# Layer 0 of a four-layer graph network: a bias, a fetch, a count array and an output stage are placed differently

## The chip, the cores and the metric

The kernel is one program on one core of a Trainium2 chip. The metric is device time in microseconds (us) of one execution, the median of several runs. Engines are named as in the profile: PE (TensorE matmuls; PEld are its weight loads), DVE (VectorE), ACT (ScalarE), POOL (GpSimd), SP (SyncE, which only issues transfers). Any of SP, ACT and POOL can issue a DMA, and each works its instructions off in order.

## The reference

The whole is four layers over 3125 nodes with 256 features and 103125 edges (50000 random ones, their reverses and 3125 loops). Only layer 0 is touched by the change. It adds an edge attention (8 heads of 32) and a linear mixer to x, then a mixture of 8 experts of which each node takes its best two:

```python
xn = _layernorm(x, axis=-1)
x = x + gnn(xn, edge_index, Wp, a_src, a_trg, Wskip, bias) + mix(xn, Wqkv, ..., bproj, ...)
x = x + ffn(_layernorm(x), gamma, beta, Wr, br, W1, b1, W2, b2)

def gnn(x, ...):
    proj = (x @ Wp.T).reshape(-1, H, FO)
    s = leaky_relu(scores_src[src] + scores_trg[trg], 0.2)
    attn = exp(s) / (segment_sum(exp(s), trg)[trg] + 1e-16)
    out = segment_sum(proj[src] * attn[:, :, None], trg)
    return elu((out + (x @ Wskip.T).reshape(-1, H, FO)).reshape(-1, H * FO) + bias)
def mix(x, ...):
    ...
    return out * gate @ Wproj + bproj
def ffn(x, ...):
    xn = (x - mu) * rsqrt(var + 1e-05) * gamma + beta
    logits = xn @ Wr + br
    top_vals, top_idx = top_k(logits, 2)
    ...
    h = gelu(xn @ W1[e] + b1[e]); y_e = h @ W2[e] + b2[e]
```

## The kernel before

The nodes are 25 tiles (NT) of 125 (TP = 125 partitions); x, xn and xT stay in SBUF (N = 3125, C = 256, P = 128, KC = 2). GROUPS are seven groups of 4, 4, 4, 4, 3, 3, 3 tiles; `part_dma` splits every transfer by partitions in two. Layer 0 runs in these stages.

**Preparation** (0 to 102 us). `run` loads x in four parts, in turns over SP and ACT; `begin` normalises and transposes group by group; `prepare` projects each group for the attention and, at group 3, calls `edges()`, which turns the sorted edge list into keys (`is_key`, `seg_d` in DRAM).

**Counts** (102 to 377). The graph is turned into a dense table: how many edges run from each source node to each target node. `counts` makes 63 steps: DVE compares keys to two one-hot tables (`oh_lo` L1734, `oh_key` L1737), PE multiplies these (`p_cnt` L1750), ACT evicts the sums to `stage` (L1752) or, for the targets in FAR, also to `far` (L1755). Each block of 250 targets is written to the DRAM arrays `count_d` (bytes, L1759) and `far_d` (bf16, L1762) by SP. BLOCKS is the order of the blocks. Between the steps, 93 pieces of the mixer are woven in (`mix0_pieces`): first node tables, then the fold (`fold_pieces`, which loads wkv at L1627), then for each group the gated output. Ahead of the groups POOL adds `bproj` to the whole of x at once (L1786).

**Attention loop** (`dense_pairs`, 387.7 to 1012.4). Every pair of nodes is weighed by its count. The instruction order is written out by hand (`manual_schedule`). A near step n handles one (block, head) unit and one of 25 source tiles (NS = 25): DVE makes `pt` from the row `q_here`, the source's scalar `bar` and the counts `a` in one instruction over 1000 targets (L1986), PE multiplies it with the sources' features (L2000). There are 16 units, that is 400 near steps: the 8 heads for target tiles 0 to 7, then the 8 heads for tiles 8 to 15. A far step m does the nine tiles 16 to 24 (FAR0) for a pair of heads without DVE: ACT computes leaky relu and exp (L2029, L2030), POOL multiplies by the counts (L2031), PE sums (L2045). There are 100 far steps, one for every four near ones. When a unit is through, its sums are evicted (L1965) and turned to node rows (`turned`, L1954 to 1960); after the eighth head of the first block `then` (`outputs0`) is put into the list `ends`. `piece()` advances the open `turns` and then `ends` by one yield in each near step. After the loop the other eight near tiles and the nine far tiles go through `outputs0` alone.

**Outputs** (`outputs0`). For each tile: Wskip and the skip bias on PE (helper `mm`, L740; the bias is a matmul of one row of ones with one row of bias), added to the attention on DVE (L2696), ELU (exp and relu on ACT L2700, L2701; then DVE L2688, L2689, which also brings the result into x), batch-norm statistics. For all tiles: a root on ACT (L2704), `xn` normalised on DVE (L2711) and written to DRAM, transposed on PE (L2717), scaled into xT on DVE (L2719), multiplied with Wr for 8 scores a node (L2727, two matmuls a tile), then the best two by DVE.

**Experts** (from 1114). `routed0_weights` loads W1, b1, W2, b2 (L2755, 2757, 2759, 2663) over ACT and SP; `route` sorts nodes by expert; `routed0` gathers xn's rows with POOL (L2782), multiplies, and scatters results (L2848). Then layer 1 starts.

## Time and profile before

| what | us |
|---|---|
| median of 7 runs | 5538.43 (5535.86 to 5552.24) |
| the profiled execution's own time | 5542.23 |
| its span in the trace | 5540.3 |

| stage (us from the span's start) | length | PE busy | DVE busy | ACT busy | POOL busy | granted clock |
|---|---|---|---|---|---|---|
| preparation, 0 to 102 | 102.0 | 70.17 | 66.69 | 26.34 | 13.54 | 0.88 |
| counts, 102 to 377 | 275.0 | 235.59 | 239.69 | 180.27 | 21.26 | 0.91 |
| attention loop, 387.7 to 1012.4 | 624.7 | 596.84 | 536.69 | 515.29 | 476.38 | 0.97 |
| last outputs, 1012.4 to 1114.1 | 101.7 | 80.57 | 52.21 | 18.65 | 0 | 0.52 |
| route, 1114.1 to 1146.7 | 32.6 | 12.69 | 19.26 | 0 | 7.36 | 0.50 |
| first 238.3 us of the experts | 238.3 | 232.72 | 134.49 | 37.89 | 106.80 | 0.99 |

How to read it: the table's lines are busy times of engines by stretch, and "granted clock" is the TensorE clock that the throttle allowed, as a share of full speed. A line of the timeline in the text below has start, duration, engine, program line, operation, output<-inputs, shape, how many such instructions were put together, and in square brackets how long the engine was idle before it and what it then waited for. A line of the waits gives the waiting engine and line, what it waited for, and total us, number and longest. A line of the groups gives engine, operation, shape and count, then busy us and mean ns of one, then the idle time before.

### The profile page before, as it was taken

The numbers are of one execution on the slowest core, as the hardware profiler recorded it, in microseconds if no ns is written. First come the engines' busy times: TensorE is split into PE (matmuls) and PEld (weight loads), VectorE is DVE, ScalarE is ACT, GpSimd is POOL, SyncE is SP. The second block draws the span as 40 slices with busy tenths as digits, with TensorE's granted clock in tenths as the row PEclk, the third lists the DMA queues.
The fourth block names the chain that finished last, engine by engine and source line by source line (L and its number), as shares of the span: only waits on it lengthen the run. The fifth ranks groups of instructions, "written<-read, shape, count | busy, mean of one in ns | idle before, by whom it ended". The sixth has DMA issues, their size and how long they took to land. (4 is left out here: it accounts for less than half of the span.)

```text
span 5540.3 us, 68126 instructions
## 1 busy us (share of the span) xinstructions
PE 4836.3 (87%) x24840; PEld 2897.2 (52%) x24840; DVE 3530.0 (64%) x5869; ACT 1575.4 (28%) x2503; POOL 1520.8 (27%) x1398
## 2 busy tenths in 40 slices
PE   6889989889888999899998999999967668686768
PEld 4565434568444333686453334556645445454447
DVE  6978888555655998454448997323267666565643
ACT  3668868311421000101330001333311012222221
POOL 1118858234000000000100000000066556555533
PEclk8899999689899999999999999999978889888889
DMA  3865535412200111110001112000055455444535
GB/s 90 91 91 157 162 108 161 130 49 62 69 1 25 34 35 27 51 36 14 14 1 35 44 29 69 14 0 1 27 150 145 127 151 159 129 138 141 143 117 175
DMA packets 353191, 443.06 MB, mean 80 GB/s; under 512 B 144846, under 2 KB 273229, under 8 KB 352278
## 3 DMA queue, kind: packets, MB, share of 16 engines
q1 hardware_dynamic: 264514, 219.66, 16.4%
q0 software_dynamic: 53744, 171.34, 10.8%
q10 hardware_dynamic: 34593, 47.63, 2.8%
q8 instruction: 202, 3.31, 0.2%
q14 instruction: 138, 1.13, 0.1%
HBM read 384.86 MB, written 56.78 MB: 80 GB/s over the span
## 5 line engine op out<-in xcount | busy, mean ns | idle before, releaser
L2289 POOL DMA_INDIRECT z_edge<-tab,src_i x806 | 771.3, 957 | 535.2 <-issue 214.6
L1905 DVE SCALAR_TENSOR_TENSOR pt<-q_head,bar,a 128x750 f32<-128x750 f32 (+2 forms) x800 | 776.6, 1027 | 62.2 <-PE acc L2135 53.6
L2130 PE MATMUL acc<-pt,zs 128*64 128x375 f32 (+2 forms) x3200 | 603.5, 501 | 24.0 <-DVE pt L1905 23.8
L2357 PE MATMUL p_acc<-z_edge,oh 128*125 128x264 f32 x2044 | 557.4, 435 | 41.0 <-DVE z_edge L2348 25.4
L2031 POOL TENSOR_TENSOR pt_far<-pt_far,a_far 128x1125 f32<-128x1125 f32 (+1 forms) x200 | 476.4, 2383 | 279.8 <-ACT pt_far L2030 248.6
L2357 PEld LDWEIGHTS p_acc<-z_edge,oh 128*125 128x125 f32 x2044 | 435.8, 217 | 142.1 <-DVE z_edge L2348 28.0
L1986 DVE SCALAR_TENSOR_TENSOR pt<-q_here,bar,a 128x1000 f32<-128x1000 f32 (+1 forms) x384 | 456.0, 1250 | 40.2 <-DMA a<-count_d 18.0
L2130 PEld LDWEIGHTS acc<-pt,zs 128*64 128x64 f32 (+1 forms) x3200 | 246.9, 136 | 357.2 <-issue 220.8
L2000 PE MATMUL p_n<-pt,zs 128*64 128x500 f32 (+1 forms) x1600 | 402.8, 597 | 26.4 <-DVE pt L1986 25.7
L1278 DVE SCALAR_TENSOR_TENSOR x<-p_y,sm,x 125x256 f32<-125x256 f32 x200 | 96.7, 483 | 364.5 <-PE p_y L740 364.5
L2135 PE MATMUL acc<-pt,zs 128*32 128x375 f32 (+2 forms) x3200 | 313.4, 497 | 0.0
L2348 DVE TENSOR_TENSOR z_edge<-z_edge,near_e 128x2112 f32<-128x2112 f32 (+1 forms) x101 | 236.6, 2342 | 120.1 <-ACT near_e L2340 71.4
L2324 PE MATMUL p_e<-ident,m_sb 128*128 128x128 f32 x202 | 52.3, 348 | 282.2 <-ACT m_sb L2319 185.0
L2185 PE MATMUL acc<-zs,pt 128*125 128x257 f32 x1250 | 275.8, 383 | 11.6 <-DMA a<-count_d 11.6
L2185 PEld LDWEIGHTS acc<-zs,pt 128*125 128x125 f32 x1250 | 234.8, 189 | 52.6 <-issue 14.4
L2000 PEld LDWEIGHTS p_n<-pt,zs 128*64 128x64 f32 (+1 forms) x1600 | 159.2, 137 | 183.8 <-issue 79.1
L2029 ACT ACTIVATE pt_far<-q_log,log_s 128x1125 f32<-128x1125 f32 (+1 forms) x200 | 244.8, 1224 | 32.7 <-PE p_f L2045 30.7
L2045 PE MATMUL p_f<-pt_far,zs 128*64 128x375 f32 (+1 forms) x1200 | 242.6, 489 | 7.9 <-POOL pt_far L2031 7.8
L2030 ACT ACTIVATE pt_far<-pt_far,log_s 128x1125 f32<-128x1125 f32 (+1 forms) x200 | 247.0, 1235 | 6.5
L1262 ACT ACTIVATE h<-p_tr,bn 128x500 f32<-128x500 f32 (+1 forms) x224 | 161.8, 723 | 299.4 <-PE p_tr L740 299.4
L2319 ACT ACTIVATE m_sb<-p_m 128x256 f32<-128x256 f32 x101 | 38.8, 384 | 711.1 <-remote 350.5
L2302 DVE TENSOR_TENSOR hot<-row,near 125x1024 f32<-125x1024 int16 (+1 forms) x149 | 158.6, 1083 | 78.5 <-remote 64.6
(550 smaller groups left out, 7841.5 us busy)
## 6 DMA issues: line engine op xcount, KB each, us to landing
a<-count_d SPq DMA_DIRECT2D x384, 125.0 KB
a_far<-far_d SPq DMA_DIRECT2D x96, 281.2 KB
row<-dst_row SPq DMA_DIRECT2D x101, 224.0 KB
a<-count_d SPq DMA_DIRECT2D x144, 93.8 KB
ef<-in_edge_s SPq DMA_DIRECT2D x101, 128.0 KB
z_edge<-tab,src_i POOLq DMA_INDIRECT x806
count_d<-stage SPq DMA_DIRECT2D x12, 781.2 KB
q_head<-q_g ACTq DMA_DIRECT2D x24, 375.0 KB
```

The source lines that it names most:

```text
L1905: self.nc.vector.scalar_tensor_tensor(pt[:K, :n], q, bar, a[:K, :n], op0=OP.max, op1=OP.mult)
L1986: nc.vector.scalar_tensor_tensor(pt[:K], q[:K], bar[:K, t, h:h + 1], a[:K].rearrange("p (j n) -> p j n", j=2), op0=OP.max, op1=OP.mult)
L2000: nc.tensor.matmul(accs[u][64 * j:64 * j + 64, :M * TP], zs[:K, t, h * W:h * W + 64], pt[:K, j, :], start=(t == 0), stop=(t == NS - 1))
L2029: nc.scalar.activation(f[:K], logs[u, i][:K], AF.Relu, bias=log_s[:K, 0, t, h])
L2030: nc.scalar.activation(f[:K], f[:K], AF.Exp, bias=log_s[:K, 1, t, h], scale=1.0 - 0.2)
L2031: nc.gpsimd.tensor_tensor(f[:K], f[:K], a[:K], OP.mult)
L2045: nc.tensor.matmul(far_accs[u][b][64 * i:64 * i + 64, :n], zs[:K, t, z:z + 64], fs[i][:K, b * n:(b + 1) * n], start=(t == 0), stop=(t == N ...
L2130: nc.tensor.matmul(acc[i // 2][64 * (i % 2):64 * (i % 2) + 64, b, :b1 - b0], zs[:K, t, i * W:i * W + 64], pts[i][:K, b0:b1], **st)
L2135: nc.tensor.matmul(acc[2][32 * i:32 * i + 32, b, :b1 - b0], zs[:K, t, z:z + 32], pts[i][:K, b0:b1], **st)
L2185: nc.tensor.matmul(acc[i], pt[:K, i * TP:(i + 1) * TP], zs[:K, t, :C + 1], start=(t == 0), stop=(t == NS - 1))
L2289: nc.gpsimd.indirect_dma_start(out=zs[i][:, j, :], out_offset=None, in_=table, in_offset=bass.IndirectOffsetOnAxis(ap=src[:, c0 + j:c0 + j ...
L2357: nc.tensor.matmul(acc[t], ohs[i, t][:, k - a, :], zs[i][:, k - c0, :HW], start=(k == cols[t][0]), stop=(k == cols[t][1] - 1))
```

## The change

- x is loaded in the seven GROUPS, and `edges()` is called at the last group.
- BLOCKS has another order; `count_d` becomes three DRAM arrays of 1000, 1000 and 1125 targets (PARTS), so that a load of counts spans one or more arrays; the last block's counts are written by ACT's queue, not SP's.
- wkv is fetched within the node pieces, ahead of the weights that follow them.
- The addition of `bproj` to all of x goes; instead `shift = bproj - 1` is added to x tile by tile, on POOL, one tile in each of the first 25 far steps (`ahead`). The -1 is that of ELU, so that `outputs0` adds xn to x without it.
- The skip bias is a matmul of 128 rows: one row of bias and 127 of zeros, against 128 rows of ones.
- A far step comes every 3.5 near steps; the far tiles' `outputs0` joins `ends` inside the loop, and `ends` advance only in every third near step while far steps remain (`rare`).
- In `outputs0` normalisation and scaling into xT move from DVE to ACT, and the scores are computed as 8 rows by up to 500 nodes, evicted to `side` by ACT, and transposed back.
- Several pools have `reuse_waits="tile"` (waits for reused memory by tile); the experts' W1 is loaded over POOL's queue, b1, W2 and b2 over SP's.

```diff
-BLOCKS = [8, 0, 9, 1, 10, 2, 11, 3, 12, 4, 5, 6, 7]
+BLOCKS = [8, 0, 1, 9, 2, 10, 3, 4, 11, 5, 12, 6, 7]
+PARTS = ((0, 1000), (1000, 2000), (2000, N))
...
     def gnn0_weights(self, c):
...
+        bias = c.tile([P, C], F32, name="bias_row")
+        nc.gpsimd.memset(bias, 0.0)
+        nc.scalar.dma_start(bias[:1], dview(self.ins["L0_gnn_bias"], 0, [[0, 1], [1, C]]))
+        shift = self.row(c, "L0_mix_bproj")
+        nc.vector.tensor_scalar(shift, shift, -1.0, None, op0=OP.add)
...
-                if group == GROUPS[3]:
+                if group == GROUPS[-1]:
                     found = edges()
...
-        self.count_d = self.dram.tile([NS, P, N], U8, name="count_d")
+        self.count_d = [self.dram.tile([NS, P, b - a], U8, name=f"count_d{i}") for i, (a, b) in enumerate(PARTS)]
...
-                    nc.sync.dma_start(self.count_d[:, :, d0:d0 + nd].rearrange("t p d -> p t d"), stage[:, :, :nd])
+                    part = min(d0 // 1000, 2)
+                    c0 = d0 - PARTS[part][0]
+                    (nc.scalar if step == steps - 1 else nc.sync).dma_start(
+                        self.count_d[part][:, :, c0:c0 + nd].rearrange("t p d -> p t d"), stage[:, :, :nd])
...
-            for _ in self.node_pieces(nodes[:3], "g0", xT, 8, 0.2, w, ps, nodes[3:]):
+            for i, _ in enumerate(self.node_pieces(nodes[:3], "g0", xT, 8, 0.2, w, ps, nodes[3:])):
+                if i == len(GROUPS) + NS:
+                    wkv = self.keys_weight(w, "gate")
                 yield
...
-            nc.gpsimd.tensor_add(x, x, bproj[:, None, :].to_broadcast([TP, NT, C]))
...
-        nc.sync.dma_start(a[:K, :n], self.count_d[t, :K, d0:d0 + n])
+        for part, (c0, c1) in zip(self.count_d, PARTS):
+            b0, b1 = max(c0, d0), min(c1, d0 + n)
+            if b0 < b1:
+                nc.sync.dma_start(a[:K, b0 - d0:b1 - d0], part[t, :K, b0 - c0:b1 - c0])
...
-                        ends.append(then(we, ps_t, c, nn))
+                        ends.append(then(we, ps_e, c, nn))
...
+                    if 2 * u + 2 == H:
+                        ends.append(then(we, ps_e, f0, nf))
...
-                    if m <= NF and n >= 4 * m:
+                    if m <= NF and n >= 3.5 * m:
...
+                        if m < NT:
+                            ahead(m)
                         m += 1
...
-                    piece()
-                while turns or ends:
+                    piece(n % 3 and m <= NF)
+                while turns:
                     piece()
                 in_loop.close()
-                last = s.enter_context(tc.tile_pool(name="dapl", bufs=8, space=PSUM, reuse_waits="tile"))
-                ends = [then(we, last, n0 + nn, nn), then(we, last, *FAR0)]
+                banks.append(room("dapl", 7, space=PSUM))
+                ends.append(then(we, ps_e, n0 + nn, nn))
                 while ends:
                     ends = [e for e in ends if next(e, self) is not self]
...
-                self.mm(ys[k], [(xT[:, i, t * TP:(t + 1) * TP], wskip[:, i, :]) for i in range(KC)] + [(self.ones[:1, :TP], bias)])
+                self.mm(ys[k], [(xT[:, i, t * TP:(t + 1) * TP], wskip[:, i, :]) for i in range(KC)] + [(self.ones[:, :TP], bias)])
...
-                nc.vector.scalar_tensor_tensor(x[:, t, :], xn[:, t, :], -1.0, x[:, t, :], op0=OP.add, op1=OP.add)
+                nc.vector.tensor_add(x[:, t, :], x[:, t, :], xn[:, t, :])
...
+        nc.vector.scalar_tensor_tensor(off[:, :nt], mv[:, :nt, 0], -1.0, rstd[:, :nt], op0=OP.mult, op1=OP.mult)
...
-                nc.vector.tensor_scalar(xn[:, t, :], x[:, t, :], mv[:, k, 0:1], rstd[:, k:k + 1], op0=OP.subtract, op1=OP.mult)
+                nc.scalar.activation(xn[:, t, :], x[:, t, :], AF.Identity, bias=off[:, k:k + 1], scale=rstd[:, k:k + 1])
...
-                nc.vector.tensor_scalar(xT[:, k, (t0 + a) * TP:(t0 + a + na) * TP], p[:, :na * TP], g[:, k:k + 1], b[:, k:k + 1],
-                                        op0=OP.mult, op1=OP.add)
+                nc.scalar.activation(xT[:, k, (t0 + a) * TP:(t0 + a + na) * TP], p[:, :na * TP], AF.Identity, bias=b[:, k:k + 1], scale=g[:, k:k + 1])
...
-        for t in range(nt):
-            self.mm(p[:, t, :], [(xT[:, k, (t0 + t) * TP:(t0 + t + 1) * TP], wr[:, k, :]) for k in range(KC)])
+            p = ps.tile([P, 512], F32, name="p_o")[:E, :na * TP]
+            self.mm(p, [(wr[:, k, :], xT[:, k, (t0 + a) * TP:(t0 + a + na) * TP]) for k in range(KC)])
...
+            nc.scalar.activation(side[32 * i:32 * i + E, :na * TP], p, AF.Copy)
...
+        for u in range(each):
+            nc.tensor.transpose(p[:, u, :], side[:, u * TP:(u + 1) * TP], self.ident)
...
-                (nc.sync if e % 2 else nc.scalar).dma_start(w1[:, k, :, e, :], ins["L0_ffn_W1"][e, k * P:(k + 1) * P].rearrange("p (i f) -> p i f", i=2))
+                nc.gpsimd.dma_start(w1[:, k, :, e, :], ins["L0_ffn_W1"][e, k * P:(k + 1) * P].rearrange("p (i f) -> p i f", i=2))
...
-            nc.scalar.dma_start(b1[:, i], dview(ins["L0_ffn_b1"], i * C, [[0, P], [2 * C, E], [1, C]]))
+            nc.sync.dma_start(b1[:, i], dview(ins["L0_ffn_b1"], i * C, [[0, P], [2 * C, E], [1, C]]))
...
-            (nc.scalar if e % 2 else nc.sync).dma_start(w2[:, :, e, :], ins["L0_ffn_W2"][e].rearrange("(k p) f -> p k f", p=P))
-        return w1, w2, b1, self.matrix_rows(c, "L0_ffn_b2")
+            nc.sync.dma_start(w2[:, :, e, :], ins["L0_ffn_W2"][e].rearrange("(k p) f -> p k f", p=P))
+        return w1, w2, b1, self.matrix_rows(c, "L0_ffn_b2", nc.sync)
...
-        for i, (t0, nt) in enumerate(((0, 4), (4, 4), (8, 8), (16, 9))):
+        for i, (t0, nt) in enumerate(GROUPS):
...
+                                 lambda t: nc.gpsimd.tensor_add(x[:, t, :], x[:, t, :], skip[-1]))
```

## The prediction

> **What bounds it now.** Read first: busy time and granted TensorE clock by stretches (columns: stretch; its length; busy us of PE, PEld, DVE, ACT, POOL with instruction counts; clock; DMA share; GB/s). All edits sit in layer 0: preparation 0 to 102 us, counts to 377, attention loop 387.7 to 1012.4, a serial tail to 1146.7, then the experts.
>
> ```profile
> 388.00:700.00 312.00, 302.62 (x1539) 151.74 (x1540) 265.01 (x255) 276.15 (x243) 258.62 (x108) 0.98 0.56 163
> 700.00:780.00 80.00, 72.29 (x318) 27.07 (x320) 70.87 (x90) 52.17 (x58) 42.38 (x18) 0.94 0.36 102
> 780.00:830.00 50.00, 43.95 (x210) 18.45 (x212) 43.94 (x54) 29.26 (x27) 27.43 (x12) 0.86 0.39 114
> 830.00:1012.00 182.00, 177.58 (x915) 85.61 (x913) 156.56 (x149) 157.01 (x139) 147.95 (x63) 1.00 0.50 146
> 1012.00:1018.00 6.00, 3.10 (x18) 1.57 (x14) 2.14 (x9) 1.52 (x3) 0.00 (x0) 0.92 0.50 153
> 1030.00:1050.00 20.00, 20.00 (x39) 10.35 (x38) 7.72 (x22) 4.47 (x11) 0.00 (x0) 0.50 1.01 329
> 1050.00:1072.00 22.00, 22.00 (x43) 11.49 (x42) 13.03 (x38) 6.45 (x16) 0.00 (x0) 0.50 0.00 0
> 1072.00:1080.00 8.00, 0.22 (x1) 0.00 (x0) 7.45 (x24) 3.46 (x7) 0.00 (x0) 0.50 0.00 0
> 1148.00:1152.00 4.00, 3.49 (x12) 2.43 (x12) 1.39 (x4) 0.70 (x1) 0.95 (x1) 0.72 0.11 34
> ```
>
> In the loop (first four rows) PE is full and DVE, ACT and POOL are close behind it. From 700 to 830 PE starves while DVE is full: there the first 8 output tiles run inside the loop. The next rows are the tail, where 17 output tiles run alone: PE is busy throughout at clock 0.50, from 1072 DVE works alone. At 1148, with the experts' 128-row matmuls, the clock rises again.
>
> Second, one tail tile in order of time:
>
> ```profile
> 1042.74 1.21 PE L740 MATMUL p_o<-r_L_gnn_bias,ones 1*125 1x256 f32 x2
> 1043.89 2.07 PE L740 MATMUL p_o<-w_L_gnn_Wskip,xT 128*125 128x256 f32 x4
> 1043.99 0.42 DVE L2696 TENSOR_TENSOR xn<-xn,p_o 125x256 f32<-125x256 f32 x1 [2.63 <-PE p_o L740]
> ```
>
> A tile costs 1.21 + 2.07, overlapped 3.14 us, and DVE waits 2.63 of it. So PE sets the pace there; the bias, one row deep, is over a third.
>
> Third, the counts stage and the loop's start, in order of time:
>
> ```profile
> 154.98 13.73 POOL L1786 TENSOR_TENSOR x<-x,r_L_mix_bproj 125x6400 f32<-125x6400 f32 x1 [49.31 <-DMA r_L_mix_bproj<-in_L_mix_bproj]
> 155.06 14.98 DVE L1737 TENSOR_TENSOR oh_key<-key_t,is_key 128x2520 bf16<-128x2520 bf16 x1
> ...
> 387.67 1.26 DVE L1986 SCALAR_TENSOR_TENSOR pt<-q_head,bar,a 128x1000 f32<-128x1000 f32 x1 [11.02 <-DMA a<-count_d]
> 392.74 8.26 DVE L1986 SCALAR_TENSOR_TENSOR pt<-q_here,bar,a 128x1000 f32<-128x1000 f32 x7 [3.81 <-DMA a<-count_d]
> ```
>
> One POOL addition of 13.73 holds a DVE comparison of 1.46 for 14.98. The loop's first two vector steps wait 11.02 and 3.81 for counts.
>
> Fourth, the waits of that stage (us, times, longest):
>
> ```profile
> DVE oh_lo L1734 <- PE p_cnt L1750: 12.7, 15, 5.3
> ACT far L1755 <- DMA far_d<-far: 12.2, 2, 6.7
> ```
>
> PE and DVE stall behind ACT, which waits until the single far buffer has been written out.
>
> Fifth, DVE groups (count | busy, mean ns): first inside the loop (690 to 826), then in the tail.
>
> ```profile
> L2689 DVE SCALAR_TENSOR_TENSOR x<-xn,x 125x256 f32<-125x256 f32 x8 | 11.4, 1424 | 0.3
> L2711 DVE TENSOR_SCALAR xn<-x,mv,rstd 125x256 f32<-125x256 f32 x8 | 10.8, 1409 | 0.0
> ...
> L2689 DVE SCALAR_TENSOR_TENSOR x<-xn,x 125x256 f32<-125x256 f32 x17 | 7.2, 425 | 0.6
> L2711 DVE TENSOR_SCALAR xn<-x,mv,rstd 125x256 f32<-125x256 f32 x17 | 5.9, 407 | 0.1
> ```
>
> Beside POOL the same operation takes 1424 instead of 425, 1409 instead of 407.
>
> **The sum, part by part.** Times are those of the profiled execution, 5542.2 (span 5540.3), 3.8 above the median 5538.4.
>
> Preparation: the edge work moves to the last group and x comes in 14 pieces, not 8. DVE sat idle for 6.62 before the edge data (56 to 62.8), with later layernorms queued behind it; these now fill it. But the edge work, 14.5 on DVE, comes nearer to the end. Bounds 0 (all back) and -15 (all of it off the chain); I take -6, about the idle alone. Six more x issues cost 0.35 to 0.8 each on SP and ACT, under transfers that take 15.
>
> Counts: DVE is busy 239.7 of 275, so it paces. Without the addition: -13.5, but PE has 36 us of work in the 36 us left between 150 and 200, so -11. The new block order puts two or three blocks between most far writes instead of two: half of the 12.7. The Wkv fetch moves a few pieces earlier on POOL's queue; behind it stand only small memsets, so nothing. Bounds -8 and -24; -17.
>
> Loop start: the loads of the first counts need not wait for the last write, which leaves SP for ACT. The mixer's last addition ends at 376.6, so at most 11.02 + 3.81 = 14.8 go; the 500 KB query row still shares the DMA engines with that write. Bounds -6, -14.8; I take -10.
>
> Loop: steady, four near and one far step take 5.25: near 0.84 of PE, far 1.89. At 3.5 near to one far, 25 far steps need of PE 87.5 x 0.84 + 25 x 1.89 = 121, and 11 for drains (100 near steps took 142.9 where 131.3 are worked): 132. ACT needs 25 x 2 x (1.224 + 1.235) = 123, 5.6 for near and 1.4 for far evictions, 2 for new rows: 132. POOL needs 119, and 13.7 more in the first round for the 25 additions: 133. With three engines equal I take 136; bounds 132, 143. Near steps 0 to 206: 320; 300 to 350: 78. Between, 94 steps: 146, plus the first outputs. These bring PE 17.5 (8 tiles of 1.65, transposes, scores), ACT 15 (ELU 0.84, norm 0.42, evictions 0.3 a tile, two table loads), DVE 31 of which 11 is waiting for POOL; against some 5, 5 and 30 free: +20 (bounds 5, 40), 166. The last 50 near steps have no far work: DVE 50 x 1.19, turns 3.8, nine far tiles of 1.85: 80. Together 644 against 624.7 - 3.8: **+23**. The normalisation on ACT takes away the 1409s; ACT has no slack for it, which is why I grant little.
>
> The Trainium skill ("SBUF — State Buffer", SBUF: two separate sides) says a DVE operation with two SBUF inputs and a GpSimd operation that reads SBUF lock each other out; that speaks against POOL additions in the loop. By it, all 25 of 0.55 could stand in DVE's way: 14 more. The rows allow less: the near step, with one operand in PSUM, takes 1250 beside a POOL that is 83% busy.
>
> Tail: far tiles go through their ELU part in the loop (28 of 53 pieces, after 16 for far and near turns and 6 for the next). Left: last turn 3.2; eight tiles at DVE's 0.41 + 0.40 + 0.43 + 0.43 + 0.18 = 1.85, with start and lag 19; far top-two 4.6; root with its table 2.3; ACT norms, transposes, evictions and score matmuls (two 500-wide pairs and four transposes for 14.3 of 8-wide ones) 10.5; top-two 4.5. Sum 44 where 1012.4 to 1114.1 is 101.7: -57, taken -56. PE hides under DVE only if the clock is full: 1.65 a tile; at half, 3.14 stays and the sum is 54, so -47. I take full, since the bias is now 128 rows deep and 128-row matmuls bring the clock back at 1148.
>
> By the Trainium skill ("TensorE: Matmul & The Clock Gate", What's actually happening) some 3.4 us of busy time restore full clock whatever the rows. The rows here contradict it: 42 us busy at 0.50. By the rule the bias edit would win no clock.
>
> Expert weights: the loads leave ACT for POOL (16) and SP (11). Before, the DMA had finished by 1050, 37 after issue. On POOL the nearest row is 512 KB issued at 216.7, used at 224.1: eight such are 59, and the first use comes about 74 after the loop. The gathers queue behind them on POOL and xn's writes behind the others on SP; at worst 10 late. Route's constants ready earlier: -1.5. In later layers 100 count loads are split in two, 0.3 us of SP each, under 4 us steps: nothing.
>
> Sum: -6 - 17 - 10 + 23 - 56 - 1.5 = -67.5: 5474.7, less 3.8: **5471**.
>
> **Rivals.** (a) The loop does not lengthen: PE's own sum, 596 busy before, grows by only some 10. Loop 0, total -90: 5448. Against it: ACT is already 88% busy.
> (b) Covers fail: clock stays half, preparation gains nothing, gathers late: -67.5 + 9 + 6 + 10 = -42: 5496. For it: the clock fell at 1017 after a mere 3 us of idle PE.
> (c) Slower: the far chain (ACT, POOL, PE in turn, four buffers) paces the loop and does not fill. The change decides for worse where a far step over the first 350 near steps exceeds 136/25 + 67.5/100 = 6.1 us. For it: 7.7 from 700 to 824 (16 far steps). Against: there DVE held near steps at 2.1, and elsewhere it ran at 5.7. At 6.4: +30, 5568.
> (d) The parts cancel, within 10.
>
> **Numbers.** Forecast 0.66, (a) 0.15, (b) 0.08, (c) 0.08, (d) 0.03. 0.2% is 11 us, about what a measurement here can tell. Low: loop 0, preparation -12, counts -20: -110, 5428. High: loop +45, tail -47, counts -11, preparation 0, start -6: -20, 5518. Both reach (a) and (b). Faster 0.89, same 0.03, slower 0.08.
>
> **What would show it.** No POOL addition of 13.7 and no 15 us comparison; first near step under 385; far steps near 5.4 and near-only steps at 1.2 at the end; ACT, not PE, ending the far waits; 45 to 55 from the last near matmul to route, clock near 1 there. Wrong if far steps exceed 6.1, if the tail stays above 80, or if counts still take 265.

## The result, and the profile after

The changed kernel takes 5580.08 us (median of 24 runs) against 5546.29 for the kernel before (61 runs): a ratio of 1.0057, 95% interval 1.0044 to 1.0069. It is slower by 0.6%, where 1.2% faster was forecast. Runs were made in several groups; in two of them, both on one chip, the edge attention of layer 3, which no edit touches, took 1044 to 1055 us (from its first gather to its last product), in the others, on other chips as far as the chip is on record, 1314 to 1345. So whole times are compared only within a group, as ratios to the kernel before, and stages are read from the profiles.

The profiled execution of the changed kernel has its own time 5579.92 and a span of 5578.1. Stages, in us, against the first profile before ("key comparison" is the DVE step that makes `oh_key`; near steps are counted from 0, and all times are starts):

| stage | before | after | difference | forecast |
|---|---|---|---|---|
| start to first key comparison | 121.1 | 107.6 | -13.5 | -6 |
| first to last key comparison (counts) | 246.2 | 261.6 | +15.4 | -17 |
| last key comparison to near step 10 | 36.5 | 34.6 | -1.9 | -10 |
| near step 10 to last near step | 604.0 | 674.1 | +70.1 | +23 |
| last near step to first expert matmul | 138.9 | 84.1 | -54.8 | -57.5 |
| sum, layer 0 to the first expert matmul | 1146.7 | 1162.0 | +15.3 | -67.5 |

The remaining 22.5 of the span's 37.8 lie behind layer 0. Layer 3 alone is 31.0 longer (1313.5 to 1344.5), the rest somewhat shorter. The kernel before, profiled three times, had 1313.5, 1055.4 and 1317.7 there, and with the bproj addition left out 1344.8, so this part is not read as an effect of the change. Layer 0 itself varies too: in eight further profiles at one far step for 3.5 near ones the first expert matmul came at 1157.2 to 1185.4, in three of the kernel before at 1140.7 to 1158.4. So the +15.3 is at the low end. Behind the first expert matmul, the eight profiles of the two groups with the short layer 3 lie within 8 of each other (4128 to 4136), the kernel before among them (4130). So layer 0 is where the 0.6% most likely comes from; no run separates it further.

Busy time and clock by stretches of the changed kernel (columns as before: stretch, length, busy PE, PEld, DVE, ACT, POOL, clock, DMA share, GB/s):

```profile
404.00:711.00 307.00, 289.85 (x1456) 131.10 (x1454) 251.14 (x230) 269.44 (x237) 273.74 (x132) 0.98 0.51 147
711.00:997.00 286.00, 259.11 (x1227) 100.84 (x1225) 224.08 (x240) 231.41 (x222) 203.72 (x88) 0.95 0.43 125
997.00:1078.00 81.00, 70.12 (x284) 24.01 (x282) 78.02 (x112) 14.48 (x30) 2.48 (x2) 0.96 0.30 79
1084.00:1102.00 18.00, 17.29 (x75) 10.86 (x75) 10.32 (x30) 13.49 (x28) 9.68 (x14) 1.00 1.00 327
1102.00:1114.00 12.00, 1.72 (x7) 0.89 (x6) 9.43 (x34) 4.86 (x10) 2.94 (x7) 0.67 1.07 370
1132.00:1150.00 18.00, 6.03 (x29) 3.98 (x29) 15.49 (x45) 0.99 (x1) 0.00 (x0) 0.50 0.00 0
```

The first row is the loop without outputs, the second with the first eight output tiles, the third the near steps that are left when the far steps are through. In neither of the first two is an engine full: PE has 0.94 and 0.91 of the time, where it had 0.97 before in the stretch without outputs and 0.90 and 0.88 in those with them. The last three rows are the tail: the clock is at 1.00 while the eight tiles run, then DVE works alone.

One tail tile in order of time, as before the change at 3.14:

```profile
1089.89 1.03 PE L742 MATMUL p_o<-w_L_gnn_Wskip,xT 128*125 128x256 f32 x4
...
1091.39 0.42 DVE L2716 TENSOR_TENSOR xn<-xn,p_o 125x256 f32<-125x256 f32 x1 [1.81 <-PE p_o L742]
...
1092.38 0.59 PE L742 MATMUL p_o<-bias_row,ones 128*125 128x256 f32 x2
```

Wskip takes 1.03 instead of 2.07, the bias, now 128 rows, 0.59 instead of 1.21, both at the full clock; the Wskip of successive tiles starts every 1.4 to 3.0.

Counts and loop start in order of time:

```profile
188.68 8.49 POOL L1883 COPY log_s<-es 128x200 f32<-128x200 f32 x1 [94.54 <-DVE es L1879]
...
205.88 0.83 POOL L1635 DMA_DIRECT2D gate<-in_L_mix_Wqkv  x1 [7.91 <-ACT far L1762]
...
213.63 5.29 PE L742 MATMUL p_a<-gate,xT 128*125 128x512 f32 x6 [7.09 <-DMA gate<-in_L_mix_Wqkv]
...
224.85 1.49 DVE L1741 TENSOR_TENSOR oh_lo<-lo_t,is_lo 128x2560 bf16<-128x2560 bf16 x1 [11.29 <-PE p_cnt L1757]
...
378.44 1.25 DVE L2002 SCALAR_TENSOR_TENSOR pt<-q_head,bar,a 128x1000 f32<-128x1000 f32 x1
391.30 1.26 DVE L2002 SCALAR_TENSOR_TENSOR pt<-q_here,bar,a 128x1000 f32<-128x1000 f32 x1 [11.60 <-DMA count_d<-stage]
```

The addition of 13.7 is gone, but a POOL copy of 200 columns lasts 8.49, the matrix "fetched ahead" is issued behind it and after 7.91 more of waiting, PE waits 7.09 for it and DVE 11.29 for PE. The first near step comes 9.2 earlier than before, and then the second waits 11.60.

The waits of the counts, and the groups of DVE and ACT, first inside the loop (715 to 1000), then in the tail:

```profile
DVE oh_lo L1741 <- PE p_cnt L1757: 22.6, 19, 11.3
...
ACT far L1762 <- DMA far_d<-far: 4.9, 1, 4.9
```

```profile
L2709 DVE TENSOR_TENSOR x<-x,xn 125x256 f32<-125x256 f32 x8 | 9.2, 1156 | 0.8
L2708 DVE SCALAR_TENSOR_TENSOR xn<-elu_e,xn 125x256 f32<-125x256 f32 x8 | 7.5, 936 | 0.0
L2736 ACT ACTIVATE xn<-x,off,rstd 125x256 f32<-125x256 f32 x8 | 4.1, 585 | 0.0
...
L2709 DVE TENSOR_TENSOR x<-x,xn 125x256 f32<-125x256 f32 x8 | 3.4, 425 | 0.3
L2708 DVE SCALAR_TENSOR_TENSOR xn<-elu_e,xn 125x256 f32<-125x256 f32 x8 | 3.4, 420 | 0.1
```

DVE's wait for PE grew from 12.7 to 22.6, while ACT's for `far_d` fell from 12.2 to 4.9. In the loop the sums of the outputs still take 0.9 to 1.2 instead of 0.42; the normalisation on ACT takes 0.585.

### The profile page after: what moved, and what is told of

The parts are those of the page before. It is cut to its first block, busy times and chain, and to the rows that moved or that the text cites. A ratio compares the mean times of both kernels' runs of the same rounds, so it can differ in the third digit from the quotient of the medians.

```text
span 5578.1 us, 68201 instructions
## 1 busy us (share of the span) xinstructions
PE 4825.8 (87%) x24779; PEld 2842.3 (51%) x24779; DVE 3521.9 (63%) x5834; ACT 1598.8 (29%) x2549; POOL 1542.9 (28%) x1442
## 5 line engine op out<-in xcount | busy, mean ns | idle before, releaser
L2150 PE MATMUL acc<-pt,zs 128*64 128x375 f32 (+2 forms) x3200 | 604.0, 502 | 23.8 <-DVE pt L1915 23.6
L2377 PE MATMUL p_acc<-z_edge,oh 128*125 128x264 f32 x2044 | 556.7, 435 | 40.2 <-DVE z_edge L2368 22.6
L2016 PEld LDWEIGHTS p_n<-pt,zs 128*64 128x64 f32 (+1 forms) x1600 | 138.0, 139 | 238.4 <-DVE pt L2002 110.8
## 6 DMA issues: line engine op xcount, KB each, us to landing
ef<-in_edge_s SPq DMA_DIRECT2D x101, 128.0 KB
```

Source lines behind the costliest of these rows:

```text
L2016: nc.tensor.matmul(accs[u][64 * j:64 * j + 64, :M * TP], zs[:K, t, h * W:h * W + 64], pt[:K, j, :], start=(t == 0), stop=(t == NS - 1))
L2150: nc.tensor.matmul(acc[i // 2][64 * (i % 2):64 * (i % 2) + 64, b, :b1 - b0], zs[:K, t, i * W:i * W + 64], pts[i][:K, b0:b1], **st)
L2377: nc.tensor.matmul(acc[t], ohs[i, t][:, k - a, :], zs[i][:, k - c0, :HW], start=(k == cols[t][0]), stop=(k == cols[t][1] - 1))
```

## Experiments

Differences to the kernel before or the changed kernel are given as short diffs.

### Is layer 3, and the low clock of the tail, the change's doing?

**before_again** and **before_third** are the kernel before, unedited.

> The kernel before once more, to see how far the stages differ between two executions. Layer 3's instructions are the same and in the same order in both kernels, but its first 30 edge chunks took 24 us longer in the changed kernel's profile. If that is chance, this run's first 30 chunks also differ from the 400.7 of the first profile, by 10 or more; if the change causes it, they stay within 5 of 400.7. Layer 0 up to the first expert matmul should be within 3 of 1146.7.

Measured: layer 3 took 1055.4 instead of 1313.5, its first 30 chunks 328 instead of 401. It is not constant for one and the same kernel; the 24 that those chunks took longer in the first comparison is no evidence. Layer 0 came 11.7 later (1158.4) where at most 3 was expected; 9.8 of it arose ahead of near step 10.

> The kernel before a third time. First to last key comparison took 246.2 and 252.6 in its two profiles and 257 to 278 in those of the changed kernel. If the chip sets most of that difference, this run lies at 250 to 262; if the change does, at 246 to 253. If the half clock in the last outputs is the kernel's own, the tail is 138 to 140 again; if it is chance, 121 to 123 may come as in before_no_addition.

Measured: counts 250.3, tail 121.8 with the clock at full:

```profile
1035.00:1062.00 27.00, 24.51 (x88) 13.67 (x86) 17.44 (x50) 9.35 (x25) 0.00 (x0) 1.00 0.99 323
```

The kernel before, with its one-row bias, ran these 17 tiles at 0.50 in two of its profiles (tail 138.9 and 139.6) and at 1.00 here. before_no_addition, below, had 121.9. So 17 of the 55 that the tail lost in the first comparison can come without any edit.

**bias_one_row**, the changed kernel with

```diff
-[(self.ones[:, :TP], bias)]
+[(self.ones[:1, :TP], bias[:1])]
```

> The changed kernel with the skip bias as a one-row matmul again. Theory A (rows keep the clock up): the clock falls to 0.50 in the tail while the eight tiles run, a tile takes 3.1 instead of 1.9, and from the last near step to the first expert matmul it takes 92 to 98 instead of 84 to 85. Theory B (the clock stays up because the matmuls follow the loop without a gap): clock 0.9 or more over the eight tiles, 84 to 87.

Measured: tail 84.8, clock 1.00. One row or 128 makes no difference here, and Theory B's numbers hold; its reason, matmuls that follow the loop without a gap, is not shown by this. In all 16 profiles with the new outputs, this one among them, the half clock around the tail's start gave way to the full one within 3.4 to 10.2, where the old outputs kept it in two of four. Whether some edit makes this more reliable was not tested.

```profile
1100.00:1126.00 26.00, 22.07 (x91) 11.25 (x89) 13.13 (x39) 15.99 (x33) 12.47 (x19) 1.00 0.90 308
```

### The counts

**before_no_addition**, the kernel before without

```diff
-            nc.gpsimd.tensor_add(x, x, bproj[:, None, :].to_broadcast([TP, NT, C]))
```

> The kernel before without POOL's addition of bproj to x (that part of x is left out). Theory A (the 13.7 of POOL that held DVE hid other waits, above all that for the single hg buffer, which shows as a step of 10 to 12 in the changed kernels): first to last key comparison shrinks by 0 to 4 from 246 to 253, and a step of 8 or more appears near step 14. Theory B (the addition cost what it held): it shrinks by 11 to 14, to 232 to 242.

This kernel leaves bproj out of x. Measured: first to last key comparison 255.8, more than in the three profiles of before (246.2 to 252.6). Nothing was gained. The step of 13 stands where the addition had stood, but the wait is another one than Theory A named:

```profile
167.99 1.07 ACT L1755 ACTIVATE far<-p_cnt 128x500 bf16<-128x500 f32 x2 [11.50 <-DMA far_d<-far]
168.63 1.42 PE L1750 MATMUL p_cnt<-oh_key,oh_lo 128*128 128x125 bf16 x12 [10.03 <-ACT far L1755]
...
170.09 1.49 DVE L1734 TENSOR_TENSOR oh_lo<-lo_t,is_lo 128x2560 bf16<-128x2560 bf16 x1 [10.15 <-PE p_cnt L1750]
```

ACT waits for the single far buffer to be written out, PE for ACT, DVE for PE. This wait had run under the addition, which held DVE from 155.06 to 170.04 in the first profile of before:

```profile
159.78 1.07 ACT L1755 ACTIVATE far<-p_cnt 128x500 bf16<-128x500 f32 x2 [6.70 <-DMA far_d<-far]
```

In before_again and before_third the same wait took 9.51 and 9.72 and ended at 164.30 and 167.09, while DVE was held until 167.38 and 169.94. So the wait ended 10, 3 and 3 ahead of the held comparison; that nothing at all was gained is one profile's finding, with which log_s_on_act, below, agrees.

**wkv_late**:

```diff
-                if i == len(GROUPS) + NS:
-                    wkv = self.keys_weight(w, "gate")
...
+            wkv = self.keys_weight(w, "gate")
             wq = w.tile([P, KC, C], F32, name="gwt_g0")
```

> The changed kernel with the wkv fetch back at its old place, at the start of the fold. Theory A (the fetch is not ahead: it waits on POOL for the log_s copies and for the single gate buffer, is issued 7.5 before its first use, and PE, put in order as if the matrix were there, stands 7.1 with the count matmuls behind it): the two comparisons' steps 28 to 30 of the counts shrink from 17 to 21 down to 6 to 9, and first to last key comparison from 262 to 275 down to 250 to 264; the whole is 8 to 14 lower than the changed kernel. Theory B (PE's work, not this wait, paces the counts): the step shrinks but the later steps lose it again, and first to last stays at 262 to 275.

Measured: the two steps 20.6 (16.3 to 21.2 in nine profiles with the fetch moved up), the counts 273.8, ratio to before 1.0054 (1.0036 to 1.0072). Neither theory's first half came: the edit does nothing. The fetch is issued behind POOL's log_s copies in both places, and then waits, 10.26 here, for the one `gate` buffer, which the write of `log_g` has to free:

```profile
206.86 0.73 POOL L1883 TENSOR_SCALAR log_s<-es 128x200 f32<-128x200 f32 x1
217.86 0.83 POOL L1635 DMA_DIRECT2D gate<-in_L_mix_Wqkv  x1 [10.26 <-DMA log_g<-gate]
```

The 7.91 of the changed kernel stands at the same place of the program and is put down to ACT there; that it is the same wait is read from the program, where the fetch writes the only `gate` buffer. In the changed kernel the fetch is issued 98.3 after the first key comparison, in the kernel before 95.6: it was not brought ahead.

**old_block_order**, BLOCKS as before:

> The changed kernel with the old order of the count blocks. Theory A (the new order crowds count writes and evictions where the node pieces need SP, ACT and PE): first to last key comparison 250 to 262 instead of 272 to 275. Theory B (the order does what was predicted, sparing 5 to 8 of waits for far_d): 277 to 283.

Measured: 269.0, between the two; steps 13 and 23 wait 11 to 13 again, but the waits at steps 14 and 19 are gone. The order traded one set of waits for another.

**edges_at_group3**:

```diff
-                if group == GROUPS[-1]:
+                if group == GROUPS[3]:
```

> The changed kernel with the edge work back at group 3 (x still loaded in seven groups). Theory A (the late edge work shifts the preparation's leftovers into the counts): first key comparison at 118 to 124 instead of 108 to 115, first to last 255 to 266 instead of 272 to 275, so that the tenth near step comes at 410 to 422 all the same. Theory B (the gain of the preparation stands by itself): the counts stay at 270 to 276 and the tenth near step comes at 426 to 434.

Measured: first key comparison at 110.4, counts 277.9, tenth near step at 425.0. Both theories missed: the first key comparison did not move back, so the late edge work is not what the preparation gained by. What is left is x in seven groups or another edit ahead of the counts; it was not separated further.

**one_count_array**, `PARTS = ((0, N),)`:

> The changed kernel with one count array again instead of three (the last write stays on ACT's queue). From the last key comparison to the tenth near step the changed kernels took 36.1 to 38, the kernel before 37.9 and 39.5. Theory A (the loads of counts wait in any case, for the landing of the last write whose completion semaphore they share in turn, and for the DMA engines that this write fills): 36 to 40, the three arrays are worth under 2. Theory B (the arrays free the first loads): 42 to 48.

Measured: 36.0, where the changed kernels with three arrays took 34.4 to 36.7. Theory A: the three arrays are worth under 2.

**log_s_on_act**, built on outputs_after_loop below:

```diff
-            nc.gpsimd.tensor_copy(logs[0][:, 0], es)
-            nc.gpsimd.tensor_scalar(logs[0][:, 1], es, slope - 1.0, None, op0=OP.mult)
+            nc.scalar.activation(logs[0][:, 0], es, AF.Copy)
+            nc.scalar.activation(logs[0][:, 1], es, AF.Copy, scale=slope - 1.0)
```

> As outputs_after_loop, but the two log_s copies ahead of the wkv fetch run on ACT instead of POOL. Theory A (the 8.5 copy on POOL holds back the fetch behind it, and the fetch holds PE and DVE): the fetch is issued 6 to 10 sooner against the first key comparison, PE's wait falls from 12.4 to 2 to 6, first to last key comparison from 257.7 to 246 to 252, and the whole is 5 to 10 below outputs_after_loop against its own kernel before (0.9938 to about 0.992). Theory B (the counts are paced by the DMA writes, and the wait's time comes back at the next write): first to last stays within 4 of 257.7.

Measured: PE's wait for the matrix fell from 12.4 to 0.2, counts 251.4 (before_third, beside it, 250.3), ratio 0.9924 (0.9906 to 0.9943). The sizes are Theory A's, but its mechanism is not: the fetch is issued 98.9 after the first key comparison, as in ratio4_no_block_add (98.7), where the copies stand directly before it. What differs is the transfer, 4.2 from issue to first use against 12.9. In ratio4_no_block_add a count and a far write are issued 5 ahead of the fetch (203.8 and 204.2, the fetch 209.2), here 4 behind it (213.3 and 213.7, the fetch 209.6). So the DMA engines were filled by these writes in the one and free in the other; 210 to 215, ratio4_no_block_add first, then this kernel (the last figure but one is the DMA engines' busy share):

```profile
210.00:215.00 5.00, 0.00 (x0) 0.00 (x0) 5.00 (x9) 0.87 (x3) 0.02 (x1) 0.61 1.33 94
```

```profile
210.00:215.00 5.00, 3.96 (x24) 2.78 (x23) 5.00 (x7) 4.70 (x14) 0.34 (x1) 0.50 0.49 137
```

The whole moved from 0.9938 by less than the intervals can tell.

### The loop

**early_ratio4**:

```diff
-                    if m <= NF and n >= 3.5 * m:
+                    if m <= NF and n >= (4 * m if m < 50 else 50 + 3 * m):
```

> The changed kernel, but the first 50 far steps come one for every 4 near steps and the last 50 one for every 3, so that the far steps end at near step 350 as in the changed kernel. Theory A (the far chain of ACT, POOL and PE has a pace of its own, 5.7 us a far step in both kernels between near steps 10 and 160, and does not become faster when far steps are set closer): near step 200 comes at 674 as before the change instead of 710.6, but near step 350 stays at 975 to 1000 (996.7) and the loop's end at 1055 to 1085. Theory B (the engines share work, PE needs 0.84 for a near and 1.89 for a far step, and the far chain fills up when it is asked to): near step 350 at about 930 and the loop's end about 60 sooner than 1078.

Counted from near step 10 (403.8 there, 417.4 here) near step 200 came after 274.0 (before 269.7, changed 306.8), near step 350 after 571.8 (changed 593.0), the loop's end after 654.1 (changed 674.1). Theory B's 526 for step 350 is refuted: the 50 far steps set closer took 297.8, 5.96 each. Theory A's constant 5.7 is not right either, since 20 are saved. Near steps 10 to 100, where the 25 additions stand, took 130.1 here and 150.9 in the changed kernel.

**no_shift_additions**:

```diff
-                        if m < NT:
-                            ahead(m)
```

> The changed kernel without the 25 additions of bproj - 1 on POOL (that part of x is left out). If the additions stand in the far chain's way, the far steps of the first 100 near steps take 5.45 each instead of 5.93, near step 100 comes 10 to 13 sooner (542 to 545 instead of 554.7) and the loop's end as much sooner. If the far chain's pace is set by ACT or PE alone, POOL has room for them and near step 100 moves by less than 4. By the bound that each addition stops DVE for its 0.73, 18 sooner.

This kernel leaves bproj - 1 out of x. Measured: near steps 10 to 100 took 137.2 instead of 150.9 (150.9 to 156.4 in eight profiles with the additions at this ratio), the loop 661.1 instead of 674.1; ratio to before 1.0028 (1.0014 to 1.0043). The first theory holds, and the groups say where the 13.7 were: in the four first steps of a unit, changed kernel first, then without the additions.

```profile
L2002 DVE SCALAR_TENSOR_TENSOR pt<-q_head,bar,a 128x1000 f32<-128x1000 f32 x4 | 21.5, 5372 | 1.6 <-PE p_n L2016 1.6
L2922 POOL TENSOR_TENSOR x<-x,r_L_mix_bproj 125x256 f32<-125x256 f32 x24 | 18.5, 771 | 0.0
```

```profile
L2002 DVE SCALAR_TENSOR_TENSOR pt<-q_head,bar,a 128x1000 f32<-128x1000 f32 x4 | 7.7, 1917 | 0.8 <-PE p_n L2016 0.8
```

4 x (5.372 - 1.917) = 13.8. In order of time, one of these in the changed kernel:

```profile
505.65 8.02 DVE L2002 SCALAR_TENSOR_TENSOR pt<-q_head,bar,a 128x1000 f32<-128x1000 f32 x1
...
502.08 4.61 POOL L2047 TENSOR_TENSOR pt_far<-pt_far,a_far 128x1125 f32<-128x1125 f32 x2
506.66 0.72 POOL L2922 TENSOR_TENSOR x<-x,r_L_mix_bproj 125x256 f32<-125x256 f32 x1
507.34 4.59 POOL L2047 TENSOR_TENSOR pt_far<-pt_far,a_far 128x1125 f32<-128x1125 f32 x2
511.89 0.71 POOL L2922 TENSOR_TENSOR x<-x,r_L_mix_bproj 125x256 f32<-125x256 f32 x1
513.84 2.32 POOL L2047 TENSOR_TENSOR pt_far<-pt_far,a_far 128x1125 f32<-128x1125 f32 x1 [1.23 <-ACT pt_far L2046]
```

The DVE step begins at 505.65 and ends at 513.67, 1.07 after POOL first paused, at 512.60. Only the first step of a unit has its row `q_head` in SBUF; the other 24 read `q_here` in PSUM and keep to 1250. By the Trainium skill ("SBUF — State Buffer", SBUF: two separate sides) an instruction with two SBUF inputs on DVE and one on GpSimd that reads SBUF exclude each other, each for its whole length. The traces agree, and in the cases looked at here the one that waits stays out until the other pauses. The log_s copy of 8.49 beside back-to-back comparisons is the same with the roles exchanged: it ends at 197.17, 0.2 after DVE paused. At one far step for four near ones POOL pauses more (busy 0.83 of 388 to 700 before the change, 0.89 of 404 to 711 after it), and the same 25 additions cost 2 to 6: near steps 10 to 100 took 128.0 to 131.2 with them (five profiles) and 124.9 to 126.4 without (six).

**norm_on_dve**, normalisation and scaling into xT as before:

> The changed kernel with normalisation and scaling into xT back on DVE. Theory A (ACT, full with the far chain, pays for the first outputs): near steps 200 to 350 take 268 to 278 instead of 286. Theory B (the outputs cost what they cost by their waits in order between PE, ACT and DVE, whoever normalises): 282 to 292. In the tail DVE gets 9 to 14 us of work: 88 to 98 instead of 84 to 85, if DVE paces it.

Measured: 289.8 for near steps 200 to 350: Theory B, ACT's load is not it. The tail took 79.1 where 88 to 98 was expected, so DVE does not pace all of it; normalisation on ACT, as in the change, makes the tail some 5 longer (83.3 to 85.4 in nine profiles).

**outputs_each_step**, `piece()` for `piece(n % 3 and m <= NF)`:

> The changed kernel with outputs advancing in every near step, not every third. Theory A (an output piece costs its own time wherever it stands): near steps 200 to 350 take 283 to 289 as now. Theory B (spreading makes the pieces cheaper because they find free slots): 292 to 305. Theory C (spreading makes them dearer, as each piece breaks the rhythm once): 265 to 278.

Measured: 278.2, just above theory C's 278: the spreading costs 8.

**ratio4_throughout**:

```diff
-                    if m <= NF and n >= 3.5 * m:
+                    if m <= NF and n >= 4 * m:
...
-                    piece(n % 3 and m <= NF)
+                    piece(n % 2 and m <= NF)
```

> The changed kernel with one far step for every 4 near steps to the end, outputs advancing in every second near step instead of every third, and the last outputs one range after the other. Theory A: the loop costs 400 near steps of 1.43 plus 20 to 35 for the first outputs, so its last near step comes at 985 to 1010 instead of 1078; the outputs of the nine far tiles fall behind the loop and lengthen the tail from 84 to 110 to 125; the experts' first matmul comes at 1105 to 1130 instead of 1162, the whole 30 to 55 below the changed kernel. Theory B (the loop is bound by PE's sum, whatever the order): the loop ends within 25 of 1078, and the whole is not faster, as the tail grows by more.

Measured: loop 609.5, tail 123.5, first expert matmul at 1156.5; ratio to before 1.0014 (1.0001 to 1.0027). Theory A's tail, and nearly its loop, but the stages ahead of near step 10 took 20 more than in the first profile of the changed kernel, so the first expert matmul missed its range.

### Towards a better version

**ratio4_groups** and **ratio4_old_counts** add bproj - 1 in the counts, by groups or at once; **ratio4_no_block_add** leaves it in the far steps. All three have one far step for four near ones throughout.

> The changed kernel with one far step for every 4 near ones, bproj - 1 added on POOL by groups in the counts instead of in the far steps, wkv fetched at its old place, and the far and the last near outputs interleaved after the loop. Theory A (far chain paces, additions hold it, fetch stalls PE): from near step 10 to the last near step 600 to 610 (changed 650 to 674, before 604), from there to the first expert matmul 100 to 118 (before 139), counts 250 to 264; the whole 15 to 40 below the kernel before. Theory B (the engines' sum bounds each stage, so what is taken away comes back): within 10 of the kernel before.

Measured: loop 607.8, tail 112.2, but counts 288.0: additions beside the comparisons cost 12 to 16 against the three kernels run with it. Ratio 1.0005 (0.9989 to 1.0021).

> The changed kernel with the counts stage of before (old block order, wkv fetched late, bproj - 1 added to x at once on POOL), one far step for 4 near ones, and the last outputs interleaved. If counts of before and preparation of after add up: first key comparison 108 to 115, first to last 246 to 256, start 35 to 38, loop 605 to 609, tail 110 to 114, so the first expert matmul at 1105 to 1125 and the whole 25 to 45 below the kernel before. If the preparation's gain comes back in the counts: the first expert matmul at 1125 to 1145, the whole 5 to 25 below.

Measured: counts 274.7 (with a step of 17.4 for the addition, after the far wait of 12.1), loop 603.3, tail 113.6, first expert matmul 1140.5; ratio 0.9984 (0.9963 to 1.0005): the preparation's gain comes back in the counts. Where the program's scheduling now puts the addition, it and the far wait follow each other, and both are paid.

> The changed kernel with the old block order and the old place of the wkv fetch together, one far step for 4 near ones with the 25 additions left in the far steps, and the last outputs interleaved. Theory A (block order and fetch together cost the counts some 13 us and the additions 14 where they stood in the counts): first to last key comparison 254 to 262 (changed 272 to 275), near steps 10 to 100 in 127 to 131, loop 604 to 610, tail 110 to 114, first expert matmul 1120 to 1135, the whole 15 to 35 below the kernel before. Theory B (late edge work alone costs the counts 20): first to last 268 to 276, the whole within 15 of before.

Measured: counts 256.2, near steps 10 to 100 129.7, loop 605.8, tail 114.0, first expert matmul 1119.5, ratio 0.9966 (0.9951 to 0.9982): Theory A's numbers. But norm_on_dve and outputs_each_step, run beside it with the changed counts, had 260.3 and 257.8 there, so block order and fetch are worth 2 to 4 in this group, not the 13 expected.

**outputs_after_loop** is ratio4_no_block_add with the following (and with two ranges of outputs at a time):

```diff
-                    if h == H - 1 and c == n0:
-                        ends.append(then(we, ps_e, c, nn))
...
+                ends[:0] = [then(we, ps_e, n0, nn)]
```

> As ratio4_no_block_add, but the outputs of the first eight tiles are done after the loop too, two ranges at a time interleaved. Near steps 200 to 350 took 263 to 266 with these outputs at this ratio, and 150 steps at 1.43 are 215. Theory A (outputs cost some 50 inside the loop, and 3.1 a tile outside, as the nine far tiles did: 112 less 84): near steps 200 to 350 take 214 to 222, the tail 132 to 142, the first expert matmul 15 to 30 sooner than in ratio4_no_block_add. Theory B (outside they cost as much as inside): tail 155 to 165, no gain.

Near steps 200 to 350 without and with the first outputs (ratio4_no_block_add first):

```profile
672.00:935.00 263.00, 243.34 (x1169) 95.69 (x1166) 222.15 (x250) 208.42 (x204) 175.56 (x77) 0.97 0.47 136
```

```profile
677.00:892.00 215.00, 211.03 (x1089) 98.58 (x1088) 189.82 (x187) 191.87 (x170) 177.70 (x75) 1.00 0.56 162
```

214.8 instead of 262.1: the eight tiles cost 47 inside the loop, and there PE is full again at clock 1.00. The tail grew from 114.0 to 148.4, 4.3 a tile, more than the 3.1 expected, so the first expert matmul comes 8.7 sooner, not 15 to 30. Ratio to before 0.9938 (0.9917 to 0.9959): faster than both kernels.

## Why the prediction was wrong

The forecast was 5471 and faster; it came out slower, above the range. Layer 0 missed the forecast by 82.8 in the profile (+15.3 for -67.5): 47 of it in the loop, 32 in the counts, 8 at the loop's start. By the prediction's own steps:

- **Preparation** (-6; bounds 0 and -15): -13.5, inside the bounds, but not for the reason given: with the edge work back at group 3 the gain stayed (edges_at_group3).
- **Counts** (-17): this step failed. It took the 13.7 that the addition held DVE for as time on the path, because DVE "paces" at 239.7 of 275. The addition covered the wait for `far_d`, which before_no_addition laid bare: without it nothing is gained. The prediction named that wait (12.2 in the waits) and did not ask whether it ran at the same time. The fetch, costed at nothing, was the second miss. It is not issued sooner, since it waits for POOL's copies or for the `gate` buffer, whichever ends last. From issue to first use it took 6.5 to 7.4 in the kernel before, 7.7 to 9.9 with the new block order and 12.9 to 15.1 with the old one. PE, placed as if it were there, waits 6.3 to 14.1 for it in 14 of the 16 profiles of changed kernels (not in ratio4_old_counts and log_s_on_act). With that wait down to 0.2, in log_s_on_act, the counts are back at those of the kernel before (251.4 and 250.3), not below. The new block order, costed at a gain of half of 12.7, moved waits about: old_block_order took 269.0.
- **Loop start** (-10): the first near step came 9.2 earlier, as forecast, but the second waits 11.60 and near step 10 falls at 403.8 in both profiles. "The loads of the first counts need not wait for the last write" was wrong: one array gives 36.0, three 34.4 to 36.7.
- **Loop** (644 worked out from the first near step to the last, 699.5 measured). Near steps 10 to 200: 295 worked out, 306.8 measured, 296.2 without the additions. So the rate of 5.44 for a far step holds without outputs and additions, and the additions were mis-sized: at most 4 in the sum (136 for a round where PE and ACT need 132), 13 measured over the loop. Here the prediction had the right rule in hand ("14 more") and set it aside by the row of the near step that reads PSUM; the first step of each unit does not. Near steps 200 to 350: 253 worked out (6 steps of 1.55, then 166 and 78, with +20 for the outputs in them), 286 measured. The largest miss is this term: by the same rate the first outputs cost 53, above the +20 and its bounds of 5 and 40 (47 measured at four near steps to a far one). Normalisation on ACT does not help (286.2 and 289.8 with it on DVE). A likely reason, not shown by a run, is that free time on an engine can't be used by a chain of short pieces that wait for each other in order; the spreading over every third step is 8 of it. Near steps 350 on: 80 and 81.2. The start gives the other 10.
- **Tail** (-57.5 with route): -54.8, the size right, in part by luck: 17 of it is the clock, and the profile read before the change happened to be one at half clock. The 128 rows of bias are not needed for it: one row ran at full clock, and so did the old outputs in two of four profiles (before_third and before_no_addition). What the edits give, beside a tail of 121.8 at full clock, is 38: about 28 for the nine far tiles (112.2 against 84.1 with the far tiles in the loop), the rest for the new ends of `outputs0`. The page "TensorE: Matmul & The Clock Gate" (What's actually happening) of the Trainium skill lets some 3.4 of busy time restore the clock, whatever is issued: before_third agrees, its clock was back after 3.4, and the first profile, with PE busy from 1030 to 1072 at 0.50, does not.
- **Rival (c)** is what came about. It put the switch at a far step of 6.1 over the first 350 near steps; measured are (996.7 - 378.4) / 100 = 6.18. Its reason, the far chain pacing the loop, is only part of it: without outputs and additions a far step took 5.46, as forecast, and the additions and outputs are what slow it. It got 0.08, against 0.66 for the forecast. The row that spoke for it was misread: between 700 and 824 begin 14 far steps, not 16, so one took 8.9 there and not 7.7.
- **Range**: the low end does not add up. Its parts, with -10, -56 and -1.5 for the others, give -99.5 and 5439, not -110 and 5428. The measured time lies beyond the other end, so nothing hangs on it.

Ending the far steps 50 near steps early was to be paid back by a shorter tail. It is not: in ratio4_throughout the loop is 64.6 shorter for 39.3 more in the tail, and of the tail only 28 are the far tiles when the ranges are interleaved.

What stays open: why the changed counts took 257.8 to 275.5 in seven profiles of the same code (the long ones wait longer for writes: ACT for `far_d` 8.5 and 9.3 in two of them against 4.9 in the first profile), and why layer 3 takes a quarter longer on some chips.

## What to carry to other kernels

Before a busy interval is booked as a saving, look at which waits end inside it on the other engines: the longest of them can be what remains. Before work is put on GpSimd beside VectorE, list every form of the VectorE instruction, the rare ones too, and which of their inputs lie in SBUF. Output pieces woven into a loop that keeps four engines at 0.83 to 0.97 can cost more there than after it: here 5.9 a tile inside, 4.3 outside.

## What the runs showed of the hardware

A GpSimd run without a pause kept a VectorE instruction of 1.25 waiting until it took 8.0 and 9.2, and VectorE's comparisons stretched a GpSimd copy from 1.55 (in the kernel before) to 8.49. The granted clock changes in the trace after multiples of 3.4 (in the changed kernel's tail 6.8 at half, 27.3 at full, 13.7 at half, 3.4 at full), and the same tail instructions ran at 0.50 from 1017 to the tail's end in one run of the kernel before and at 1.00 for 30.7 of it in another. The edge attention of layer 3 took from 1044 to 1345 for the same instructions, though one gather took 0.96 to 0.97 in all runs.
